# Layer 0's decays with chunk and head on 128 partitions and a chunk's 128 tokens along them

## The chip, the cores and the metric

The kernel runs on one core of one Trainium2 chip. The metric is the device time of one execution in microseconds (us), as the median of several runs. A core has five engines that work side by side, each through its own queue in a fixed order: PE (TensorE, matmuls; its weight loads are shown as PEld), DVE (VectorE), ACT (ScalarE), POOL (GpSimd) and SP (SyncE, which here issues every DMA). On-chip memory has 128 partitions: an instruction of DVE, ACT or POOL works on up to 128 partitions at once and walks along the elements of each.

## The reference, cut to what matters

Two layers on an input `x` of 2 x 512 tokens of 512 numbers. Layer 0 is a gated linear attention with decays and a feed-forward layer, layer 1 a softmax attention and a mixer whose 4 x 4 matrices go through 50 Sinkhorn iterations. The change touches the decays of layer 0's attention alone (32 heads, chunks of 128 tokens, 4 chunks to a row of the batch):

```python
dt = jax.nn.softplus(hidden_states @ Win.T + dt_bias)      # [B, L, 32]
A = -jnp.exp(A_log_bias)
g = dt * A
gc = g.transpose(0, 2, 1).reshape(B, H, NC, CHUNK)
G = jnp.cumsum(gc, axis=-1)                                # within a chunk
...
decay = jnp.where(causal, jnp.exp(G[..., :, None] - G[..., None, :]), 0.0)
y_intra = jnp.einsum('bhnij,bhnjd->bhnid', scores * decay, xc)
Glast = G[..., -1:]
k_dec = kc * jnp.exp(Glast - G)[..., None]
cstates = jnp.einsum('bhnjd,bhnje->bhnde', k_dec, xc)
chunk_decay = jnp.exp(G[..., -1])
```

For each row of the batch, head and token the kernel needs `dt` (softplus of a small projection), the running sum `G` of `dt * A` within the chunk, `exp(Glast - G) * dt`, and for each chunk `exp(Glast)`.

## The kernel before

Tokens stand on partitions in tiles of 128, so a row of the batch is 4 chunks `c`. Weights come in 256 KB tiles (`raw`, four buffers), each is split by ACT (a rounded copy, L228) and POOL (the rest, L229) into two halves, and a product takes three matmul passes (L251). Layer 0's attention runs in units of (group of 4 heads, row of the batch, chunk), 64 in all; each does `scores`, `mix`, `state`, `gate`, `turn` and `project_out`, with the projections of the next group between them. Layer 1 follows, and the Sinkhorn chains close the kernel: two on POOL with their reciprocals on DVE, and one on DVE.

The program is written in the order of the text of `tile_adaln`, and a scheduler that knows the dependencies lays each engine's queue out anew. An engine then works through its queue strictly in that order. Which instruction stands where is therefore decided when the program is built, and an edit in one place can move others.

The head of the kernel (L353 to L371) loads `x`, the modulation weights, the identity, `Win`, `dt_bias` and `A_log`, all through SP. `decays(b)` is called once for each row of the batch (L1395 and L1400), between the loads and the first projections and scores:

- For each chunk the tokens are normalised, transposed (L200), scaled into `ht` (L203), split into `hh` (L209) and `hl` (L212), and `also` multiplies `ht` by `Win` (L392): 32 heads on 32 partitions, the chunk's 128 tokens at their place among the row's 512, in the PSUM tile `zps`.
- L399 to L409 work out softplus on tiles of 32 partitions and 512 elements: `z`, `e`, `u`, `rest`, `dt`, on DVE, with three exponentials and logarithms on ACT (L78 is the helper that records them).
- L412 multiplies by `-exp(A_log)`. The running sum goes in two levels: 15 additions within blocks of 16 tokens (L415, each on 32 x 32 elements: one token of every block), 7 additions over the 8 blocks of each chunk (L420, 32 x 4), and one that adds the offsets (L421).
- `G` is written to DRAM (L424, `g_dram`), from where `scores` loads four heads of a chunk, spread to all partitions (L512, `gb`, 256 KB, 64 of them). POOL masks it (L514), ACT takes the exponential, DVE multiplies it with the scores (L527), and PE reads the product in `mix` (L567).
- `exp(Glast)` (L427 to L431) goes to DRAM and comes back spread to all partitions as `cdb`, which `state` reads as a scalar for each head (L556, L557).
- L433 to L438 make `exp(Glast - G) * dt` and `-G`, and 12 transposes of 32 x 128 (L442) bring `-G`, `dt` and that product to token-major columns, which ACT copies into `gcol` (L443).

The temporary tiles come from the pool `wk` by name, two buffers to a name. The name `z` is also that of `mix`'s tile (L571).

Of the kernel before, what the change touches and what calls it, by code (L numbers as in the profile page):

```python
# [9 lines left out]
FP = mybir.dt.float32  # L10
# [22 lines left out]
ALU = mybir.AluOpType  # L33
# [3 lines left out]
P = 128  # L37
B, L, HID = 2, 512, 512
NC = L // P
KC = HID // P  # L40
H0, KV0, D0 = 32, 8, 128
REP0 = H0 // KV0
# [10 lines left out]
def tile_adaln(ctx: ExitStack, tc: tile.TileContext, a: dict, out: bass.AP):  # L53
    nc = tc.nc
# [3 lines left out]
    small = ctx.enter_context(tc.tile_pool(name="small", bufs=4))  # L58
    wk = ctx.enter_context(tc.tile_pool(name="wk", bufs=2))
    dram = ctx.enter_context(tc.tile_pool(name="dram", bufs=1, space=bass.MemoryType.DRAM))  # L60
    psp = ctx.enter_context(tc.tile_pool(name="ps", bufs=2, space=PSUM))
# [15 lines left out]
    def act(o, i, func, **kw):  # L77
        ins = nc.scalar.activation(o, i, func, **kw)  # L78
        tc.add_manual_dep(
            ins.ins, table.ins.name,  # L80
            mybir.DependencyInfo(mybir.DependencyClass.NoSync, mybir.DependencyReason.DATA),
            reason="the activation table",
        )
        return ins.ins
# [5 lines left out]
    def keep(shape):  # L90

        m = int(np.prod(shape[1:]))
        t = room0[0:shape[0], used0[0]:used0[0] + m]
        used0[0] += m
        if len(shape) == 2:
            return t
        names = "abc"[:len(shape) - 1]
        return t.rearrange(
            f"p ({' '.join(names)}) -> p {' '.join(names)}", **{n: k for n, k in zip(names, shape[1:])}
        )  # L100
# [36 lines left out]
    anchor = {}  # L137
# [33 lines left out]
    def temp(shape, dt, name, bufs=2):  # L171
        return wk.tile(shape, dt, name=name, bufs=bufs)
# [17 lines left out]
    def norm(src, root=rsqrt_pool):  # L190
        xn = temp([P, HID], FP, "xn")
        normalised(xn, src, root)
        return xn
# [167 lines left out]
    ident = keep([P, P])  # L361
    nc.sync.dma_start(out=ident, in_=a["c_ident"])
    win = keep([P, KC, H0])
    nc.sync.dma_start(out=win, in_=a["WinT"].rearrange("(k p) h -> p k h", p=P))
    dtb = keep([H0, 1])
    nc.sync.dma_start(out=dtb, in_=a["dt_bias"])
    alog = keep([H0, 1])
    nc.sync.dma_start(out=alog, in_=a["A_log"])
    act(alog, alog, AF.Exp)
    gn = keep([P, 1])  # L370
    nc.sync.dma_start(out=gn, in_=a["gnorm"])  # L371
# [8 lines left out]

    gcol = keep([P, 3, NC, B * H0])
    ngc, dtc, wdc = gcol[:, 0], gcol[:, 1], gcol[:, 2]
    cdb = keep([P, B * H0, NC])
    g_dram = [dram.tile([H0, L], FP, name=f"g_dram{b}") for b in range(B)]
    cd_dram = [dram.tile([H0, NC], FP, name=f"cd_dram{b}") for b in range(B)]
    def decays(b):

        zps = psp.tile([H0, L], FP, name="zps")

        def also(cs, ht):  # L390
            for kc in range(KC):
                nc.tensor.matmul(zps[:, cs], lhsT=win[:, kc, :], rhs=ht[:, kc, :], start=kc == 0, stop=kc == KC - 1)  # L392

        for c in range(NC):
            modulated(b, c, norm(xin[b * NC + c], rsqrt), modT[0], 0, also=also)

        row = lambda n: temp([H0, L], FP, n)
        z, e, u, rest, dt = row("z"), row("e"), row("u"), row("rest"), row("dt")
        nc.vector.tensor_scalar(z, zps, dtb, None, ALU.add)  # L399
        nc.vector.scalar_tensor_tensor(e, z, -1.0, z, ALU.mult, ALU.min)  # L400
        act(e, e, AF.Exp)

        nc.vector.tensor_scalar(u, e, 1.0, None, ALU.add)
        nc.vector.scalar_tensor_tensor(rest, u, -1.0, e, ALU.add, ALU.subtract)
        act(dt, u, AF.Ln)
        act(u, dt, AF.Exp, scale=-1.0)
        nc.vector.tensor_tensor(rest, rest, u, ALU.mult)
        nc.vector.tensor_tensor(dt, dt, rest, ALU.subtract)
        nc.vector.scalar_tensor_tensor(dt, z, 0.0, dt, ALU.max, ALU.add)  # L409

        G = row("G")
        nc.vector.tensor_scalar(G, dt, alog, -1.0, ALU.mult, ALU.mult)  # L412
        Gb = G.rearrange("r (n i) -> r n i", i=16)
        for i in range(1, 16):
            nc.vector.tensor_tensor(Gb[:, :, i], Gb[:, :, i], Gb[:, :, i - 1], ALU.add)  # L415
        off = small.tile([H0, NC, 8], FP, name="off")
        G4 = G.rearrange("r (c n i) -> r c n i", n=8, i=16)
        nc.vector.memset(off[:, :, 0], 0.0)
        for n in range(1, 8):
            nc.vector.tensor_tensor(off[:, :, n], off[:, :, n - 1], G4[:, :, n - 1, 15], ALU.add)  # L420
        nc.vector.tensor_tensor(  # L421
            Gb, Gb, off.rearrange("r c n -> r (c n)").unsqueeze(2).to_broadcast([H0, NC * 8, 16]), ALU.add
        )
        nc.sync.dma_start(out=g_dram[b], in_=G)  # L424
        Gc = G.rearrange("r (c i) -> r c i", c=NC)
        glast = small.tile([H0, NC], FP, name="glast")
        nc.vector.tensor_copy(glast, Gc[:, :, P - 1])  # L427
        cd = small.tile([H0, NC], FP, name="cd")
        act(cd, glast, AF.Exp)
        nc.sync.dma_start(out=cd_dram[b], in_=cd)  # L430
        nc.sync.dma_start(out=cdb[:, b * H0:(b + 1) * H0, :], in_=cd_dram[b].partition_broadcast(P))  # L431

        nc.vector.tensor_tensor(  # L433
            e.rearrange("r (c i) -> r c i", c=NC), Gc, glast.unsqueeze(2).to_broadcast([H0, NC, P]), ALU.subtract
        )
        act(e, e, AF.Exp, scale=-1.0)
        nc.vector.tensor_tensor(e, e, dt, ALU.mult)
        nc.vector.tensor_scalar(G, G, -1.0, None, ALU.mult)  # L438
        for k, src in enumerate((G, dt, e)):
            tp = psp.tile([P, NC, H0], FP, name="gtp")  # L440
            for c in range(NC):
                nc.tensor.transpose(tp[:, c, :], src[:, c * P:(c + 1) * P], ident[0:H0, 0:H0])  # L442
            nc.scalar.copy(gcol[:, k, :, b * H0:(b + 1) * H0], tp)  # L443


# [59 lines left out]
    def scores(u):  # L505

        g, b, c = u["at"]
        r0 = b * H0 + g * REP0
        q, kT = u["q"], u["kT"]
        gb = wk.tile(sh4, FP, name="gb", bufs=2)  # L510
        h0 = g * REP0
        anchor["sp"] = nc.sync.dma_start(out=gb, in_=g_dram[b][h0:h0 + REP0, c * P:(c + 1) * P].partition_broadcast(P)).ins  # L512
        dec = wk.tile(sh4, FP, name="dec", bufs=2)
        anchor["pool"] = nc.gpsimd.affine_select(  # L514
            out=dec, in_=gb, pattern=[[0, REP0], [1, P]], compare_op=ALU.is_ge, fill=-1e30,
            base=0, channel_multiplier=-1,
        ).ins
        for h in range(REP0):
            anchor["act"] = act(dec[:, h, :], dec[:, h, :], AF.Exp, bias=ngc[:, c, r0 + h:r0 + h + 1])
        sps = psp.tile(sh4, FP, name="sps", bufs=2)  # L520
        if "kh" in u:
            kh, kl = u["kh"]
            passes(sps, [((kh[:, c, :], kl[:, c, :]), exact(q[:, c], "q", sh4))])
        else:
            anchor["pe"] = nc.tensor.matmul(sps, lhsT=kT[:, c, :], rhs=q[:, c], start=True, stop=True).ins
        for h in range(REP0):
            anchor["dve"] = nc.vector.scalar_tensor_tensor(  # L527
                dec[:, h, :], sps[:, h, :], dtc[:, c, r0 + h:r0 + h + 1], dec[:, h, :], ALU.mult, ALU.mult
            ).ins
        u["pr"] = dec  # L530
        if c:
            u["qg"] = gb
            act(gb, gb, AF.Exp)
            nc.gpsimd.tensor_tensor(gb, gb, q[:, c], ALU.mult)  # L534

    def state(u, st):

        g, b, c = u["at"]
        r0 = b * H0 + g * REP0
        xw = wk.tile(sh4, FP, name="xw", bufs=2)  # L540
        nc.gpsimd.tensor_tensor(  # L541
            xw, u["v"][:, c, :].unsqueeze(1).to_broadcast(sh4),
            wdc[:, c, r0:r0 + REP0].unsqueeze(2).to_broadcast(sh4), ALU.mult,
        )
        cps = psp.tile(sh4, FP, name="cps", bufs=2)
        if type(u["kt"]) is tuple:
            kh, kl = u["kt"]
            passes(cps, [((kh[:, c, :], kl[:, c, :]), exact(xw, "xw", sh4))])
        else:
            nc.tensor.matmul(cps, lhsT=u["kt"][:, c, :], rhs=xw, start=True, stop=True)  # L550
        ns = wk.tile(sh4, FP, name="st", bufs=2)
        if c == 0:
            nc.scalar.copy(ns, cps)
        else:
            for h in range(REP0):
                nc.vector.scalar_tensor_tensor(  # L556
                    ns[:, h, :], st[:, h, :], cdb[:, r0 + h, c:c + 1], cps[:, h, :], ALU.mult, ALU.add  # L557
                )
        return ns

# [864 lines left out]
    for n, u in enumerate(units):  # L1425
        g, b, c = u["at"]
# [128 lines left out]
```

## Time and profile before

| what | value |
|---|---|
| median of 3 runs | 1373.19 us (1372.54 to 1374.4) |
| the profiled execution | 1368.2 us |
| its span, first to last instruction | 1366.4 us |
| PE busy | 1238.1 us, 91% |
| DVE busy | 1116.2 us, 82% |
| ACT busy | 842.4 us, 62% |
| POOL busy | 792.2 us, 58% |
| mean granted TensorE clock | 0.961 |
| DMA packets | 94,243, 109.81 MB |

The profile is of one execution, so sums over it are made against its own 1368.2 us. A busy PE is not a PE at its peak: matmuls are pipelined, so a 512-wide one is shown with some 390 ns while the next follows after 230 ns. A row of groups shows line, engine, operation, the tile written and those read, the shape (partitions x elements), the count, then the busy us and mean ns of one, and last the idle time of the engine before them with what ended it. In a view of waits a line shows who waited for whom: us in total, times, longest. An instruction's duration includes what it waits inside the engine after it has begun.

### The profile page before, as it was taken

Reading aid. Unit: us, or ns where it says so; the run is one execution under the profiler, and the core shown is the slowest. Engines: PE = TensorE matmul, PEld = TensorE weight load, DVE = VectorE, ACT = ScalarE, POOL = GpSimd, SP = SyncE. Lnnn points to the kernel's source line nnn. Section 1 sums busy time; section 2 is a strip of 40 time slices with the busy share of each in tenths; the row PEclk is TensorE's granted clock in tenths of the full one; section 3 lists DMA queues with packets and bytes.
Section 4 is the critical chain, followed back from the end, with each engine's and each line's share of the span. In section 5 each row is a group of like instructions: output and inputs, shape, how many; then the busy total and the mean of one; then the engine's idle time right before and its main releaser. Section 6 shows DMA issues by size and latency. Waiting matters only on the chain. (4 is left out here: it accounts for less than half of the span.)

```text
span 1366.4 us, 23105 instructions
## 1 busy us (share of the span) xinstructions
PE 1238.1 (91%) x7224; PEld 996.0 (73%) x7224; DVE 1116.2 (82%) x2732; ACT 842.4 (62%) x2378; POOL 792.2 (58%) x1233
## 2 busy tenths in 40 slices
PE   5989999999999999999999999889999999996408
PEld 2767788788788778888877787667777777764308
DVE  7999677786787777877989886788779888898887
ACT  4457476476465556666657675366758678875308
POOL 4455374265266356776788877545435855658651
PEclk9999999999999999999999999899999999997659
DMA  7122241232132233242343232623214221200001
GB/s 247 38 66 43 86 131 47 65 94 74 37 102 86 62 120 105 81 121 83 110 124 108 76 112 70 174 66 106 80 31 120 80 69 49 66 14 1 12 5 47
DMA packets 94243, 109.81 MB, mean 80 GB/s; under 512 B 13277, under 2 KB 52957, under 8 KB 94121
## 3 DMA queue, kind: packets, MB, share of 16 engines
q1 hardware_dynamic: 94120, 108.34, 27.0%
q8 instruction: 57, 0.93, 0.3%
q14 instruction: 66, 0.53, 0.1%
HBM read 100.02 MB, written 8.02 MB: 79 GB/s over the span
## 5 line engine op out<-in xcount | busy, mean ns | idle before, releaser
L870 DVE TENSOR_REDUCE m<-s 128x1 f32<-128x512 f32 x256 | 165.9, 672 | 13.4 <-PE s L866 12.7
L78 ACT ACTIVATE pt<-s 128x512 f32<-128x512 f32 x256 | 137.4, 601 | 13.0 <-PE s L904 12.0
L466 POOL TENSOR_TENSOR q<-xcos,rot 128x512 f32<-128x512 f32 x64 | 93.1, 1455 | 51.9 <-DVE xcos L464 49.2
L78 ACT ACTIVATE sg<-sg 128x512 f32<-128x512 f32 x128 | 80.9, 633 | 61.9 <-DVE sg L497 60.1
L866 PE MATMUL s<-ks,qs 96*128 96x512 f32 x256 | 104.1, 435 | 8.6 <-DVE m L870 7.2
L251 PE MATMUL pps<-hh,wq_h 128*128 128x512 f32 x256 | 103.1, 403 | 1.1 <-ACT vT L784 1.1
L251 PE MATMUL ops<-wo_h,zl 128*128 128x512 f32 x256 | 101.3, 396 | 1.0 <-DVE zl L590 0.9
L251 PE MATMUL ops<-wo_h,zh 128*128 128x512 f32 x256 | 101.3, 396 | 0.6 <-DVE zl L590 0.6
L251 PE MATMUL pps<-hl,wq_h 128*128 128x512 f32 x256 | 101.3, 396 | 0.0
L251 PE MATMUL gps<-wg_h,hh 128*128 128x512 f32 x256 | 101.1, 396 | 0.0
L534 POOL TENSOR_TENSOR gb<-gb,q 128x512 f32<-128x512 f32 x48 | 63.6, 1327 | 64.5 <-ACT gb L78 48.2
L251 PE MATMUL pps<-hh,wq_l 128*128 128x512 f32 x256 | 100.7, 394 | 0.0
L251 PE MATMUL gps<-wg_l,hh 128*128 128x512 f32 x256 | 100.7, 393 | 0.0
L904 PE MATMUL s<-qs,ks 100*128 100x256 f32 x512 | 98.9, 299 | 1.9 <-ACT pt L78 1.2
L567 PE MATMUL yps<-v,dec 128*128 128x128 f32 x512 | 94.2, 279 | 6.6 <-DVE xcos L464 2.7
L78 ACT ACTIVATE dec<-dec,room 128x128 f32<-128x128 f32 x256 | 82.7, 397 | 28.2 <-POOL dec L514 27.7
L251 PE MATMUL gps<-wg_h,hl 128*128 128x512 f32 x256 | 100.0, 391 | 0.0
L251 PE MATMUL ops<-wo_l,zh 128*128 128x512 f32 x256 | 100.0, 391 | 0.0
L514 POOL TENSOR_SCALAR_AFFINE_SELECT dec<-gb 128x512 f32<-128x512 f32 x64 | 48.4, 756 | 88.9 <-DMA gb<-g_dram 40.1
L904 PEld LDWEIGHTS s<-qs,ks 100*128 100x128 f32 x512 | 82.1, 193 | 18.3 <-ACT pt L78 5.4
L541 POOL TENSOR_TENSOR xw<-v,room 128x512 f32<-128x512 f32 x48 | 55.9, 1178 | 64.5 <-ACT v L481 64.5
L577 DVE SCALAR_TENSOR_TENSOR z<-yps,ss,sg 128x128 f32<-128x128 f32 x256 | 71.7, 342 | 26.4 <-ACT ss L78 26.0
(318 smaller groups left out, 3946.7 us busy)
## 6 DMA issues: line engine op xcount, KB each, us to landing
gb<-g_dram SPq DMA_DIRECT2D x64, 256.0 KB
raw<-in_wq SPq DMA_DIRECT2D x56, 256.0 KB
raw<-in_wg SPq DMA_DIRECT2D x48, 256.0 KB
raw<-in_wo SPq DMA_DIRECT2D x48, 256.0 KB
raw<-in_wmod SPq DMA_DIRECT2D x40, 256.0 KB
qs<-q_dram SPq DMA_DIRECT2D x64, 64.0 KB
raw<-in_wk SPq DMA_DIRECT2D x14, 256.0 KB
raw<-in_wv SPq DMA_DIRECT2D x14, 256.0 KB
```

The source lines that it names most:

```text
L78: ins = nc.scalar.activation(o, i, func, **kw)
L251: nc.tensor.matmul(ps, lhsT=l, rhs=r, start=i == 0, stop=i == n - 1)
L466: nc.gpsimd.tensor_tensor(dst, sp(xc_), sp(rot), ALU.add)
L514: anchor["pool"] = nc.gpsimd.affine_select(out=dec, in_=gb, pattern=[[0, REP0], [1, P]], compare_op=ALU.is_ge, fill=-1e30, base=0, channel ...
L534: nc.gpsimd.tensor_tensor(gb, gb, q[:, c], ALU.mult)
L541: nc.gpsimd.tensor_tensor(xw, u["v"][:, c, :].unsqueeze(1).to_broadcast(sh4), wdc[:, c, r0:r0 + REP0].unsqueeze(2).to_broadcast(sh4), ALU. ...
L567: nc.tensor.matmul(yps[:, h, :], lhsT=u["pr"][:, h, :], rhs=u["v"][:, c, :], start=True, stop=not c)
L577: nc.vector.scalar_tensor_tensor(z[:, h, :], yps[:, h, :], ss[:, h:h + 1], sg[:, h * P:(h + 1) * P], ALU.mult, ALU.mult)
L866: anchor["pe"] = nc.tensor.matmul(ps, lhsT=st["qs"][rp][0:KS, i, qt * P:(qt + 1) * P], rhs=st["ks"][s][0:KS], start=True, stop=True,).ins
L870: anchor["dve"] = nc.vector.tensor_reduce(st["m"][:, 2 * qt + s, i:i + 1], ps, AX.X, ALU.max, negate=True).ins
L904: nc.tensor.matmul(ps[:, j, :], lhsT=st["ks"][s][0:KM, kt * P:(kt + 1) * P], rhs=st["qs"][rp][0:KM, i, :], start=True, stop=True,)
```

## The change

`zps` and the temporary tiles become 128 partitions of 128 elements: partition `c * 32 + head`, a chunk's tokens along it. `also` writes the chunk's 32 heads to the partitions of the chunk, and `dt_bias` and `A_log` are loaded four times each, once for each chunk's partitions. Every DVE and ACT step of `decays` works on the new tiles; the 15 additions are on 128 x 8 elements, the 7 on 128 x 1. The step that subtracts `glast` takes it as a scalar for each partition. The 12 transposes of a row become 3 of 128 x 128. `g_dram` has a row for each chunk and head, so that four heads of a chunk lie next to each other; `cd_dram` and `cdb` have the chunk ahead of the head. The tiles get names of their own (`d_...`).

```diff
-    dtb = keep([H0, 1])
-    nc.sync.dma_start(out=dtb, in_=a["dt_bias"])
-    alog = keep([H0, 1])
-    nc.sync.dma_start(out=alog, in_=a["A_log"])
+    dtb, alog = keep([P, 1]), keep([P, 1])
+    for c in range(NC):
+        nc.sync.dma_start(out=dtb[c * H0:(c + 1) * H0], in_=a["dt_bias"])
+        nc.sync.dma_start(out=alog[c * H0:(c + 1) * H0], in_=a["A_log"])
...
-    cdb = keep([P, B * H0, NC])
-    g_dram = [dram.tile([H0, L], FP, name=f"g_dram{b}") for b in range(B)]
-    cd_dram = [dram.tile([H0, NC], FP, name=f"cd_dram{b}") for b in range(B)]
+    cdb = keep([P, NC, B * H0])
+    g_dram = [dram.tile([NC * H0, P], FP, name=f"g_dram{b}") for b in range(B)]
+    cd_dram = [dram.tile([NC, H0], FP, name=f"cd_dram{b}") for b in range(B)]
...
-        zps = psp.tile([H0, L], FP, name="zps")
+        zps = psp.tile([P, P], FP, name="zps")
...
-                nc.tensor.matmul(zps[:, cs], lhsT=win[:, kc, :], rhs=ht[:, kc, :], start=kc == 0, stop=kc == KC - 1)
+                nc.tensor.matmul(zps[cs.start // NC:cs.stop // NC], lhsT=win[:, kc, :], rhs=ht[:, kc, :], start=kc == 0, stop=kc == KC - 1)
...
-        row = lambda n: temp([H0, L], FP, n)
+        row = lambda n: temp([P, P], FP, f"d_{n}")
...
-        off = small.tile([H0, NC, 8], FP, name="off")
-        G4 = G.rearrange("r (c n i) -> r c n i", n=8, i=16)
-        nc.vector.memset(off[:, :, 0], 0.0)
+        off = small.tile([P, 8], FP, name="off")
+        nc.vector.memset(off[:, 0:1], 0.0)
         for n in range(1, 8):
-            nc.vector.tensor_tensor(off[:, :, n], off[:, :, n - 1], G4[:, :, n - 1, 15], ALU.add)
...
+            nc.vector.tensor_tensor(off[:, n:n + 1], off[:, n - 1:n], Gb[:, n - 1, 15:16], ALU.add)
+        nc.vector.tensor_tensor(Gb, Gb, off.unsqueeze(2).to_broadcast([P, 8, 16]), ALU.add)
         nc.sync.dma_start(out=g_dram[b], in_=G)
...
-        nc.sync.dma_start(out=cd_dram[b], in_=cd)
-        nc.sync.dma_start(out=cdb[:, b * H0:(b + 1) * H0, :], in_=cd_dram[b].partition_broadcast(P))
-
-        nc.vector.tensor_tensor(
-            e.rearrange("r (c i) -> r c i", c=NC), Gc, glast.unsqueeze(2).to_broadcast([H0, NC, P]), ALU.subtract
-        )
+        nc.sync.dma_start(out=cd_dram[b].rearrange("c (h o) -> (c h) o", o=1), in_=cd)
+        nc.sync.dma_start(out=cdb[:, :, b * H0:(b + 1) * H0], in_=cd_dram[b].partition_broadcast(P))
+
+        nc.vector.tensor_scalar(e, G, glast, None, ALU.subtract)
...
-            for c in range(NC):
-                nc.tensor.transpose(tp[:, c, :], src[:, c * P:(c + 1) * P], ident[0:H0, 0:H0])
+            nc.tensor.transpose(tp.rearrange("p c h -> p (c h)"), src, ident)
...
-        anchor["sp"] = nc.sync.dma_start(out=gb, in_=g_dram[b][h0:h0 + REP0, c * P:(c + 1) * P].partition_broadcast(P)).ins
+        anchor["sp"] = nc.sync.dma_start(out=gb, in_=g_dram[b][c * H0 + h0:c * H0 + h0 + REP0].partition_broadcast(P)).ins
...
-                    ns[:, h, :], st[:, h, :], cdb[:, r0 + h, c:c + 1], cps[:, h, :], ALU.mult, ALU.add
+                    ns[:, h, :], st[:, h, :], cdb[:, c, r0 + h:r0 + h + 1], cps[:, h, :], ALU.mult, ALU.add
```

More of the change, by code (lines that the diff above doesn't have):

```diff
@@ L415, in decays @@
             nc.vector.tensor_tensor(Gb[:, :, i], Gb[:, :, i], Gb[:, :, i - 1], ALU.add)
-        off = small.tile([H0, NC, 8], FP, name="off")
-        G4 = G.rearrange("r (c n i) -> r c n i", n=8, i=16)
-        nc.vector.memset(off[:, :, 0], 0.0)
+        off = small.tile([P, 8], FP, name="off")
+        nc.vector.memset(off[:, 0:1], 0.0)
         for n in range(1, 8):
-            nc.vector.tensor_tensor(off[:, :, n], off[:, :, n - 1], G4[:, :, n - 1, 15], ALU.add)
-        nc.vector.tensor_tensor(
-            Gb, Gb, off.rearrange("r c n -> r (c n)").unsqueeze(2).to_broadcast([H0, NC * 8, 16]), ALU.add
-        )
+            nc.vector.tensor_tensor(off[:, n:n + 1], off[:, n - 1:n], Gb[:, n - 1, 15:16], ALU.add)
+        nc.vector.tensor_tensor(Gb, Gb, off.unsqueeze(2).to_broadcast([P, 8, 16]), ALU.add)
         nc.sync.dma_start(out=g_dram[b], in_=G)
[L425 to L428, printed above, removed]
+        glast = small.tile([P, 1], FP, name="glast")
+        nc.vector.tensor_copy(glast, G[:, P - 1:P])
+        cd = small.tile([P, 1], FP, name="cd")
         act(cd, glast, AF.Exp)
-        nc.sync.dma_start(out=cd_dram[b], in_=cd)
-        nc.sync.dma_start(out=cdb[:, b * H0:(b + 1) * H0, :], in_=cd_dram[b].partition_broadcast(P))
-        nc.vector.tensor_tensor(
-            e.rearrange("r (c i) -> r c i", c=NC), Gc, glast.unsqueeze(2).to_broadcast([H0, NC, P]), ALU.subtract
-        )
+        nc.sync.dma_start(out=cd_dram[b].rearrange("c (h o) -> (c h) o", o=1), in_=cd)
+        nc.sync.dma_start(out=cdb[:, :, b * H0:(b + 1) * H0], in_=cd_dram[b].partition_broadcast(P))
+        nc.vector.tensor_scalar(e, G, glast, None, ALU.subtract)
         act(e, e, AF.Exp, scale=-1.0)
```

## The prediction

> **What bounds the kernel now.** I read the page first, then the busy time by stretches, then the waits of the stretch the change lies in, then VectorE's groups there. On the page PE is busy 91% of the span, so a saving on another engine counts only where PE stands idle. The stretches say where (columns: from and to, length, then busy us and instructions of PE, weight load, DVE, ACT, POOL, then granted TensorE clock, DMA share, GB/s):
>
> ```profile
> 32.00:77.70 45.70, 45.68 (x212) 35.47 (x212) 44.99 (x85) 20.56 (x42) 19.25 (x13) 0.96 0.18 52
> 77.70:106.00 28.30, 20.83 (x92) 16.08 (x93) 27.72 (x59) 14.31 (x41) 17.37 (x16) 0.88 0.22 57
> 106.00:130.00 24.00, 23.93 (x141) 20.15 (x141) 23.24 (x51) 19.07 (x66) 13.54 (x11) 1.00 0.28 59
> ...
> 200.00:300.00 100.00, 100.00 (x507) 81.42 (x506) 75.33 (x153) 57.37 (x169) 45.58 (x39) 1.00 0.23 69
> ```
>
> PE is full before 77.7 us and again after 106. Between them it misses 28.30 - 20.83 = 7.5 us, and there DVE is full (27.72 of 28.30). DVE sets that stretch. What PE waited for from 70 to 110 us:
>
> ```profile
> PE cps L251 <- DVE xcos L464: 2.1, 1, 2.1
> PE gtp L442 <- DVE G L438: 1.9, 1, 1.9
> PE yps L567 <- DVE off L420: 1.4, 1, 1.4
> PE pps L251 <- ACT vT L784: 1.1, 1, 1.1
> PE ztp L585 <- DVE dec L527: 0.9, 1, 0.9
> ```
>
> Together 7.4 us, 6.3 of it ended by DVE, twice by instructions of the decays themselves (L438, L420). The pause from 77.7 also costs clock: the TensorE clock granted from 80 to 84 us was 0.50, and eleven 512-wide matmuls followed each other at 0.43 us, where later ones take 0.23. That is 11 x 0.20 = 2.2 us. PE could thus win up to 7.4 + 2.2 = 9.6 us. From 106 us on a saving on DVE buys nothing by itself, but what was won is kept, since PE is full until about 500 us and later waits are between engines that all start earlier.
>
> **The change part by part.** *DVE.* The decays of one row are 12 wide instructions and 15 + 7 narrow ones; all keep their number. Rows from 29 to 118 us (count of both rows of the batch, busy us, mean ns):
>
> ```profile
> L415 DVE TENSOR_TENSOR G<-G 32x32 f32<-32x32 f32 x30 | 11.7, 391 | 0.5
> L420 DVE TENSOR_TENSOR off<-off,G 32x4 f32<-32x4 f32 x14 | 5.0, 356 | 0.1
> L407 DVE TENSOR_TENSOR rest<-rest,u 32x512 f32<-32x512 f32 x2 | 3.3, 1636 | 0.0
> L412 DVE TENSOR_SCALAR G<-dt,room 32x512 f32<-32x512 f32 x2 | 2.0, 982 | 0.0
> ...
> L408 DVE TENSOR_TENSOR dt<-dt,rest 32x512 f32<-32x512 f32 x2 | 1.4, 677 | 0.0
> L400 DVE SCALAR_TENSOR_TENSOR e<-z 32x512 f32<-32x512 f32 x2 | 1.4, 676 | 0.0
> ```
>
> A time here goes by elements per partition: 32x512 at L408 takes 677 ns, as 128x512 does elsewhere (L473, 672). So at 128 elements the prices are those of 128x128 rows: a tensor_tensor 0.28 us (L952, 276 ns, one input in PSUM), a scalar_tensor_tensor 0.33 (L527, 334 in the first 130 us). No 128x128 tensor_scalar exists; between 128x8 (L264, 0.16) and 32x512 (L403, 0.41) a straight line gives 0.22, and 0.29 from PSUM (L276 0.15, L399 0.73). Undisturbed savings per row of the batch: L399 0.73-0.29 = 0.44; the scalar_tensor_tensor steps L400, L404, L409 each 0.67-0.33 = 0.34; L407, L408, L421, L437 each 0.67-0.28 = 0.39; L403 0.19, L412 (0.46 at its fastest) 0.24, L438 0.18; L433 becomes a tensor_scalar, 0.67-0.22 = 0.45. Sum 0.44 + 1.02 + 1.56 + 0.61 + 0.45 = 4.1. L415 goes from 32 elements to 8: 0.20 to the 0.16 of a 128x8 tensor_tensor (L266), 15 x 0.04 = 0.6. L420 (0.148 at the median) goes from 4 to 1: nothing. That is 4.7 us a row, 9.4 for both.
>
> The means stand above the undisturbed times: 30 x (391 - 200) = 5.7 us at L415, 14 x (356 - 148) = 2.9 at L420, and about 3.4 at L407, L412 and L409. These are waits inside instructions, while POOL works. Since their number stays, I take them as staying; they are the upper end: if they go too, DVE saves 9.4 + 12.0 = 21.4, more than PE can use. The lower end is 8.2, the wide ones alone.
>
> The Trainium skill, "SBUF — State Buffer", section "SBUF: two separate sides", speaks against counting these waits: VectorE with two SBUF inputs and GpSimd hold one shared port pair by an exclusive lock for a whole instruction. By that a shorter DVE instruction waits as long for a GpSimd one as a longer one does, and the sum stays 9.4; L415's mean of 391 ns beside a minimum of 191 fits it.
>
> *How much reaches PE.* DVE's order is a queue, so savings add up from instruction to instruction. Before the pause at 77.7 us row 0 is through (4.7; its L438 is the releaser) and row 1 as far as L407 (0.44 + 0.34 + 0.19 + 0.34 + 0.39 = 1.7): 6.4 us, more than the 1.9 us pause at L438; vT's 1.1 us hang behind it (ACT's exp of gb waits for POOL, which waits for the gb load of the same G). So the first group closes: 1.9 + 1.1 + 2.2 of clock = 5.2. The second group, 2.1 + 0.9 + 1.4 = 4.4 us up to 106, is met by DVE 7.8 us ahead (6.4 plus L408, L409, L412, 0.39 + 0.34 + 0.24 = 1.0, plus eleven L415, 0.4), but PE asks 5.2 us earlier: 2.6 closes. Together 7.8.
>
> *PE.* Per row 12 transposes of 32x128 (L442) become 3 of 128x128. Row 1's lie where PE is full: G and dt, eight, take 0.7 us from 118.94 to 119.63, so twelve some 1.0; three 128x128 at L480's 0.60 for four take 0.45. Saved 0.55. Row 0's lie in the pause: nothing. The 32 zps matmuls (L392) keep number and size, only their output partitions change.
>
> *ACT.* Four 32x512 (0.63) per row become 128x128 (0.27, L573): 2.9 us on an engine busy 5 of 10 there; hidden behind PE, no gain of its own, counted at 0.
>
> *SP and the DMAs.* dt_bias and A_log are eight loads instead of two: six more issues at 0.33 to 0.43 us, 2.3 us of SP's time before 21 us. They stand before the loads of wq, wv and wg; wk and wq move behind the last wm and the identity. Queued behind them: ACT's casts (wk_h 12.17), POOL's differences, and through the four raw buffers SP again. Cover: ACT ended these casts at 15.59 and next worked at 18.59, 3.0 us. Uncovered it would cost 2.3; I take 1.0, because PE's order now puts six gate matmuls, which need wg, ahead of the first key matmuls (28.97).
>
> g_dram holds a chunk's four heads side by side, so each of the 64 gb loads is 128 pieces of 2 KB instead of 512 of 512 B (24,576 fewer of the page's 94,243 packets). POOL waited 40.1 us for gb, but PE waited only 1.7 us for POOL's gb from 110 us on. Between 0 and 1.7 us; I take 0, being hidden behind PE.
>
> The cd round trip gets smaller pieces: 4 B out, 128 B back. It was issued at 79.67 and first read by L556 at 107.18 (row 1: 112.5, read well after): 27 us of cover. Cost 0; were it late, DVE's st would stop, and PE's yps with it.
>
> The Trainium skill, "DMA: Bandwidth & Descriptors", section "Specifications", says that pieces under 512 B lose line rate to a read-modify-write. No price for four-byte pieces stands in this case's trace; by the rule this load slows, and the sum stays as long as the cover does.
>
> *Order.* The scheduler lays the program out anew, but the built programs differ only in about the first seventh of each engine's order, a few rows of the middle, and the two POOL chains (sinkhorn) of the last quarter, shifted by half an iteration. DVE's last chain starts and ends at the same places of its queue (rows 2315 to 2701 against 2314 to 2701).
>
> *Sum.* 7.8 + 0.5 - 1.0 = 7.3 us. The profiled execution took 1368.2 us (span 1366.4); it becomes 1360.9. It lies 5.0 us below the 1373.19 us median of the runs, whose least is 1372.54, so I subtract from the median: 1365.9 us, 0.53% less.
>
> **The rivals.**
> 1. *The pauses only change their owner* (no change). For it: DVE's waits for POOL (12 us) stay and PE's new order meets them elsewhere; POOL waited 15.8 us for xcos from 32 to 110 us. Against it: L438 and L420, two of the releasers, move far ahead in DVE's order. Only the transposes and a quarter of the 7.8 remain, less the loads: 0.5 + 2.0 - 1.0 = 1.5, 1371.7 us.
> 2. *More than the pauses.* POOL-held waits shrink too and the last pause closes: 9.6 + 0.5 and 1.7 of gb, 11.8: 1361.4 us.
> 3. *Slower: the last sinkhorn chain.* From 1240 us PE is no bound (54.71 of 126.4 us) and the four-tile chain on DVE is: 33 iterations, two halves each, every half with a reduce, a reciprocal and a product in series. If the new order puts one more reciprocal of the POOL chains (197 ns) ahead in each half, that is 66 x 0.197 = 13.0 us: 1365.9 + 13.0 = 1378.9 us. It decides once it takes 51 of the 66 halves. Against it: between its first and last four-tile step DVE's order holds 70 instructions of the other two chains now and 71 after.
> 4. *The change does not do what it says*: each instruction's time does not fall with 128 elements. Then nothing but the loads: about 1374. L527 at 334 ns beside L408's 677 speaks against it; I count it with the first.
>
> **How the numbers follow.** The forecast has 0.59, rival 1 (with 4) 0.16, rival 2 0.15, rival 3 0.10. The forecast's own range is 1363 to 1369.5: 7.8 may be 5.2 (the first group alone) or 9.6, the loads 0 to 2.3. The range from 1361 to 1371.9 adds rival 2 and the upper half of rival 1's cases. 0.2% is 2.7 us, about what a measurement of this kernel can tell from no change. Faster takes the forecast, rival 2 and a little of rival 1: 0.76. Same, between 1370.5 and 1375.9, the rest of rival 1: 0.14. Slower, rival 3: 0.10.
>
> **What would show it.** Right: the decays stand on 128 partitions, the wide ones are at 0.2 to 0.35 us, L415's kin at 0.16 at its fastest; PE's idle between 77 and 106 us falls below 2 us and the granted clock there stays 1.0; the first output projection comes some 7 us earlier and this lead is still there at 600 and at 1200 us. Wrong: PE's pauses stand at other lines in the same sum; the first pps after 30 us starts later than 29 us (loads); or the lead is there at 1200 us and gone at the end (sinkhorn).

## The result, and the profile after

The changed kernel is slower: 1382.66 us at the median (1382.24 to 1384.08) beside 1373.8 us (1372.54 to 1374.98) for the kernel before, a ratio of 1.0071 with a 95% interval of 1.0053 to 1.009. Beside the experiments it ran once more: 1387.63 us against 1372.48, 1.0107 (1.0081 to 1.0133). Forecast were 1365.9 us and a range of 1361.0 to 1371.9, so the time lies outside the range, on the other side of no change. The profiled execution took 1382.24 us, 14.0 more than the profiled one before (1368.2); the medians lie 8.9 us apart, for that execution was one of the faster ones of its kernel.

Where it goes is seen at the output projections. The 64 results of `project_out` leave PSUM one after the other; the 8th left at 195.8 us before and at 209.8 after, the 21st at 369.0 and 382.4, the 64th at 1026.7 and 1040.4. The lag of 14 us is complete by the 8th, and hardly anything is added or won after that.

Busy times of the same stretches as before, of the changed kernel (from and to, length, then busy us and instructions of PE, weight load, DVE, ACT, POOL, then granted TensorE clock, DMA share, GB/s):

```profile
32.00:77.70 45.70, 36.87 (x169) 27.49 (x168) 34.41 (x76) 14.26 (x35) 15.70 (x13) 0.91 0.24 50
77.70:106.00 28.30, 23.16 (x102) 17.63 (x102) 27.85 (x51) 16.72 (x49) 16.27 (x13) 0.84 0.13 40
106.00:130.00 24.00, 21.18 (x108) 17.71 (x108) 18.45 (x51) 13.97 (x50) 7.62 (x7) 0.95 0.14 40
200.00:300.00 100.00, 100.00 (x515) 81.73 (x514) 76.04 (x154) 57.04 (x165) 47.29 (x40) 1.00 0.25 75
```

The stretch up to 77.7 us, where PE had been full, now lacks 45.70 - 36.87 = 8.8 us of PE, and DVE is not full there either (34.41): both wait for something else. The pause of 77.7 to 106 fell only from 7.5 to 5.1 us, and the next 24 us miss 2.8. What PE waited for from 20 to 130 us (us in total, times, longest):

```profile
PE sps L251 <- ACT qh L466: 7.2, 1, 7.2
PE ps_tr L200 <- DVE xn L185: 4.6, 1, 4.6
PE cps L251 <- DVE d_G L416: 3.1, 1, 3.1
PE gps L251 <- ACT room L437: 2.8, 1, 2.8
```

The longest wait begins at 68.8 us. Follow it back: the first scores (`sps`) need `qh` from ACT, that needs the fourth `q` from POOL, and POOL's queue holds a mask ahead of it, `dec<-gb`, whose `gb` came late. POOL's waits, and then SP's, in the same 110 us:

```profile
POOL dec L508 <- DMA gb<-g_dram: 19.9, 3, 13.3
```

```profile
SPq L428 <- DMA cd_dram<-cd: 13.2, 2, 6.6
```

SP's issues from 60 to 76 us (start, length, line, what is moved; `room<-cd_dram` is the load of `cdb`):

```profile
61.06 0.33 SPq L422 DMA_DIRECT2D g_dram<-d_G  x1
61.70 0.33 SPq L427 DMA_DIRECT2D cd_dram<-cd  x1
62.62 1.75 SPq L506 DMA_DIRECT2D gb<-g_dram  x2
71.01 0.37 SPq L428 DMA_DIRECT2D room<-cd_dram  x1
74.14 0.32 SPq L506 DMA_DIRECT2D gb<-g_dram  x1
```

The write of the chunk decays leaves at 61.70, and the load that waits for its landing leaves 9.3 us later. In the kernel before these two stood 4.0 us apart in row 0 and 1.3 in row 1, and the first two loads of `gb` stood ahead of the write:

```profile
74.72 0.93 SPq L512 DMA_DIRECT2D gb<-g_dram  x2
75.70 0.50 SPq L430 DMA_DIRECT2D cd_dram<-cd  x1
...
79.67 0.33 SPq L431 DMA_DIRECT2D room<-cd_dram  x1
```

More than that, in the changed kernel the two loads of `gb` issued between write and load hardly move. The DMA view of 63 to 70 us, after the 128 pieces of 4 B have been sent:

```profile
DMA packets 35, 0.05 MB, mean 8 GB/s; under 512 B 9, under 2 KB 9, under 8 KB 35
```

256 packets of 2 KB were queued there and 26 moved in 7 us.

The undisturbed prices came out about as forecast. DVE's groups of the decays from 29 to 118 us (count of both rows, busy us, mean ns):

```profile
L416 DVE TENSOR_TENSOR d_G<-d_G 128x8 f32<-128x8 f32 x30 | 11.8, 394 | 0.5
L420 DVE TENSOR_TENSOR off<-off,d_G 128x1 f32<-128x1 f32 x14 | 4.9, 348 | 0.3
L413 DVE TENSOR_SCALAR d_G<-d_dt,room 128x128 f32<-128x128 f32 x2 | 2.6, 1303 | 0.1
...
L409 DVE TENSOR_TENSOR d_dt<-d_dt,d_rest 128x128 f32<-128x128 f32 x2 | 1.0, 502 | 0.0
L408 DVE TENSOR_TENSOR d_rest<-d_rest,d_u 128x128 f32<-128x128 f32 x2 | 0.9, 440 | 0.4 <-ACT d_u L78 0.4
...
L401 DVE SCALAR_TENSOR_TENSOR d_e<-d_z 128x128 f32<-128x128 f32 x2 | 0.6, 289 | 0.0
```

The scalar_tensor_tensor fell from 676 to 289 ns, the median of the wide steps is 0.29 us and the fastest L416 took 0.156. But L413, 0.98 us before, takes 1.30: what it waits for inside did not shrink.

### The profile page after: what moved, and what is told of

It reads as the page before. It is cut to its first block, busy times and chain, and to the rows that moved or that the text cites. A ratio compares the mean times of both kernels' runs of the same rounds, so it can differ in the third digit from the quotient of the medians.

```text
span 1380.4 us, 23054 instructions
## 1 busy us (share of the span) xinstructions
PE 1243.9 (90%) x7206; PEld 1000.2 (72%) x7206; DVE 1111.1 (80%) x2732; ACT 840.3 (61%) x2378; POOL 788.7 (57%) x1233
## 5 line engine op out<-in xcount | busy, mean ns | idle before, releaser
L467 DVE TENSOR_TENSOR ql<-q,qh 128x512 fp32r<-128x512 f32 x64 | 66.4, 1061 | 42.1 <-ACT qh L466 41.9
```

The source lines that it names most:

```text
L467: nc.vector.tensor_tensor(lo, src, hi.bitcast(FP), ALU.subtract)
```

## The experiments

Theory A: the write in four-byte pieces holds the DMA queue, and what stands behind it comes late. Rivals: B, the new order alone costs the time; C, the eight small loads at the start do; D, the layout's saving on DVE does not reach PE in any case. Each edit lets the scheduler lay out the program anew, except in the first experiment, whose instructions stand in the same order on PE, DVE, ACT and POOL as before; so their traces were read beside their times. In the table stands when the 8th output projection left PSUM in the profile, and the time against the kernel before in the same runs.

| kernel | 8th projection, us | median, us | before, us | ratio, 95% interval |
|---|---|---|---|---|
| before | 195.8 | | | |
| change, first / again | 209.8 / 214.8 | 1382.66 / 1387.63 | 1373.8 / 1372.48 | 1.0071 (1.0053 to 1.009) / 1.0107 (1.0081 to 1.0133) |
| e1_small_pieces | 197.3 | 1373.1 | 1372.34 | 0.9996 (0.9976 to 1.0016) |
| e2_two_loads | 212.9 | 1387.64 | 1372.34 | 1.0109 (1.0077 to 1.0141) |
| e3_cd_on_tensor | 199.7 | 1376.64 | 1372.34 | 1.0027 (1.0007 to 1.0048) |
| e4_both | 195.5 | 1374.81 | 1372.34 | 1.001 (0.9988 to 1.0032) |
| e5_one_piece | 191.6 | 1372.03 | 1372.45 | 0.999 (0.9971 to 1.001) |
| e6_sums_late | 192.0 | 1369.91 | 1372.45 | 0.9979 (0.9961 to 0.9998) |
| e7_scan | 187.1 | 1365.08 | 1372.45 | 0.9948 (0.9931 to 0.9966) |
| e8_scan_in_before | 195.4 | 1370.31 | 1372.45 | 0.9994 (0.9975 to 1.0013) |
| e9_write_behind | 204.8 | 1380.96 | 1372.48 | 1.0071 (1.0049 to 1.0093) |
| e10_piece_and_loads | 196.3 | 1373.63 | 1372.48 | 1.0015 (0.9998 to 1.0033) |
| e11_scan_late | 189.1 | 1368.78 | 1372.48 | 0.9973 (0.9953 to 0.9993) |
| e13_rotations_first | 193.9 | 1370.87 | 1373.5 | 0.9994 (0.9976 to 1.0011) |
| e14_scan_rotations_first | 187.0 | 1362.42 | 1373.5 | 0.9928 (0.9906 to 0.9949) |

Single executions of one kernel lie up to 8 us from their median, so a row is read by its interval. The lead or lag at the 8th projection, of one execution, agrees with the difference of the medians to within some 5 us in every row, so most of what an edit does here is decided by then. Not all of it shows at the end of a single execution: e5 leads by 4.2 us at the 8th projection and by 0.2 at the 64th; its granted clock in the two stretches from 800 to 1000 us was 0.93 and 0.92, that of the kernel before 0.95 and 0.97.

**e1_small_pieces.** The kernel before with the pieces of the change's round trip.

```diff
-    cd_dram = [dram.tile([H0, NC], FP, name=f"cd_dram{b}") for b in range(B)]
+    cd_dram = [dram.tile([NC, H0], FP, name=f"cd_dram{b}") for b in range(B)]
...
-        nc.sync.dma_start(out=cd_dram[b], in_=cd)
+        nc.sync.dma_start(out=cd_dram[b].rearrange("c h -> h c"), in_=cd)
```

> The kernel before with one thing of the change alone: the 128 chunk decays of a row leave VectorE's 32 partitions as 128 pieces of 4 B (32 of 16 B before) and come back as pieces of 128 B (512 B before). The order of the instructions on all engines is that of the kernel before. Theory A (the four-byte write lands late and holds what is queued behind it): the load of cdb, which SP issued 3.4 us after waiting in all, waits 6 us or more for each of the two writes, the next load of gb leaves 4 to 6 us later, and the time rises by 1 to 4 us, to 1375 to 1378. Theory B (the pieces are harmless, the order alone costs the time): SP waits no longer than before and the time stays within 1 us of 1373.8. Theory C (the eight small loads): as B.

SP's issues of row 0 and row 1 in its trace:

```profile
74.48 0.50 SPq L430 DMA_DIRECT2D cd_dram<-cd  x1
75.09 0.38 SPq L219 DMA_DIRECT2D raw<-in_wq  x1
81.53 0.36 SPq L431 DMA_DIRECT2D room<-cd_dram  x1
...
109.71 0.33 SPq L430 DMA_DIRECT2D cd_dram<-cd  x1
115.00 0.38 SPq L512 DMA_DIRECT2D gb<-g_dram  x1
118.01 0.38 SPq L431 DMA_DIRECT2D room<-cd_dram  x1
```

From write to load 7.1 and 8.3 us instead of 4.0 and 1.3, in an unchanged order: the pieces alone make the write land late. SP waited 8.5 us in all for it (3.4 before), 6.0 and 2.5, so the second wait fell short of the 6 us expected of each. The time did not move, against theory A's 1 to 4 us: in this order the loads of `gb` that PE needs first stand ahead of the write. What stands 0.6 us behind it in row 0 is a load of weights (`raw`, 128 pieces of 2 KB), and that was not held at all. The DMA view of 75 to 79 us:

```profile
DMA packets 1211, 0.73 MB, mean 182 GB/s; under 512 B 192, under 2 KB 1082, under 8 KB 1210
```

The 1210 - 1082 = 128 packets of 2 KB and more are that whole load. So a late landing alone costs nothing here, and not everything queued behind such a write stands still.

**e2_two_loads.** The changed kernel, the 32 values of `dt_bias` and `A_log` repeated four times by the host and loaded at once.

```diff
-    for c in range(NC):
-        nc.sync.dma_start(out=dtb[c * H0:(c + 1) * H0], in_=a["dt_bias"])
-        nc.sync.dma_start(out=alog[c * H0:(c + 1) * H0], in_=a["A_log"])
+    nc.sync.dma_start(out=dtb, in_=a["dt_bias"])
+    nc.sync.dma_start(out=alog, in_=a["A_log"])
```

> The changed kernel with dt_bias and A_log in one load of 128 values each, which the host repeats four times; nothing else. With two loads the order of PE begins like that of the kernel before again: the first key matmul stands ahead of the gate matmuls. Theory A (four-byte write): only the pause of 4.6 us at 25 to 30 us and some 2 us of half clock behind it go, the pauses from 70 us on stay: 1376 to 1379. Theory B or C (the order or the loads at the start are the whole of it): 1364 to 1368, as forecast for the change.

The pause of 4.6 us for row 1's normalised rows falls to 1.3, as expected, and no time is won: PE waits 12.7 us for rotations instead, SP 17.7 us for the write, and the ratio is that of the change itself. The 1387.64 us lie above every range given, theory A's too. Theory C falls.

**e3_cd_on_tensor** and **e4_both.** No round trip through DRAM; e4 adds the two loads of e2.

```diff
-        nc.sync.dma_start(out=cd_dram[b].rearrange("c (h o) -> (c h) o", o=1), in_=cd)
-        nc.sync.dma_start(out=cdb[:, :, b * H0:(b + 1) * H0], in_=cd_dram[b].partition_broadcast(P))
+        cps = psp.tile([P, NC, H0], FP, name="gtp")
+        nc.tensor.matmul(cps.rearrange("p c h -> p (c h)"), lhsT=cd.to_broadcast([P, P]), rhs=ident, start=True, stop=True)
+        nc.scalar.copy(cdb[:, :, b * H0:(b + 1) * H0], cps)
```

> The changed kernel without the round trip of the chunk decays through DRAM: one matmul of 128x128 with the identity lays them on all partitions, ScalarE copies them out. Eight loads as in the change, so PE's order begins with the gates. Theory A: SP no longer waits 13.2 us for the write, gb lands within 4 us of its issue, the pause of 7.2 us at 70 us goes and with it those of 4.6 and 2.8 us from 90 us on at least in part: 1369 to 1375, while the pause at 25 us stays. Theory B or C: 1380 to 1383, no change.

> Both: two loads and the chunk decays by TensorE. Theory A with the order at the start: the sum of both, 1362 to 1368, below both kernels, with PE's pauses from 20 to 130 us below those of the kernel before. If the layout itself brings nothing (theory D: DVE's savings do not reach PE), 1371 to 1374, as the kernel before.

With the round trip the 7.2 us pause goes; from 209.8 the 8th projection comes to 199.7, and the time to 1376.64, somewhat above theory A's range. Both edits together bring the kernel back to where it was before and not below it: e4's 1374.81 is just above theory D's 1371 to 1374. Its longest waits of PE from 20 to 130 us:

```profile
PE pps L251 <- DVE xcos L458: 5.3, 2, 3.3
PE ttp L474 <- DVE dec L521: 3.5, 1, 3.5
```

**e5_one_piece.** The round trip stays, but the decays leave as one row of 512 B.

```diff
+        rowp = psp.tile([P, NC, H0], FP, name="gtp")
+        nc.tensor.transpose(rowp.rearrange("p c h -> p (c h)")[0:1], cd, ident)
+        cdr = small.tile([1, NC * H0], FP, name="cdr")
+        nc.scalar.copy(cdr, rowp.rearrange("p c h -> p (c h)")[0:1])
-        nc.sync.dma_start(out=cd_dram[b].rearrange("c (h o) -> (c h) o", o=1), in_=cd)
+        nc.sync.dma_start(out=cd_dram[b].rearrange("c (o h) -> o (c h)", o=1), in_=cdr)
```

> The changed kernel, eight loads and round trip of the chunk decays kept, but TensorE turns the column of 128 decays into one row first, so that it leaves as one piece of 512 B instead of 128 of 4 B (the load back in pieces of 128 B stays). Theory A (the four-byte pieces of the write hold the queue): as with the decays laid out by TensorE, 1373 to 1378, SP's wait for the write falls from 13.2 us to 4 or less, and gb's first wait on POOL falls from 13.3 to below 6 us. Theory B2 (the round trip itself, or the order of SP's queue with the load of cdb in it, costs the time): 1380 to 1384, as the change.

This is the largest single step: 0.999 against the change's 1.0071 and 1.0107, some 11 to 16 us; the median, 1372.03, lies just below theory A's range. SP's wait for the write is 0.7 us, POOL's longest for `gb` 5.7. The first loads of `gb`, from 64 to 71 us of its trace:

```profile
DMA packets 415, 0.75 MB, mean 108 GB/s; under 512 B 49, under 2 KB 50, under 8 KB 414
```

415 packets in these 7 us, where the change moved 35. One thing moved beside the pieces: the row is ready later, so that the write stands behind three loads of `gb` and not ahead of two. The next run has the four-byte pieces behind two loads; behind all three they were not run, so e5 alone does not part the pieces from their place.

**e9_write_behind.** The change's own pieces, with the write behind two loads of `gb` (an order given to the scheduler), the load of `cdb` behind a third.

```diff
+            if n == 0:
+                chunk_decays(*d0)
+                chunk_decays(*d1)
...
+        tc.add_manual_dep(out_cd, anchor["sp"].name, order_only, reason="behind the second gb")
```

> The changed kernel with all its pieces, 128 of 4 B for the write and of 128 B for the load, but in SP's queue the write of the chunk decays stands behind the first two loads of gb and not ahead of them, and the load of cdb behind the third. POOL's order stays. Theory A1 (the four-byte write delays what the queue carries behind it, and it was the first gb loads that PE could not wait for): 1371 to 1377, POOL's wait for gb falls from 13.3 us at its longest to below 7. Theory A2 (the pieces cost their time wherever they stand): 1379 to 1384.

SP in its trace, and then the DMA views of 63 to 67 us and of 67 to 74:

```profile
62.50 1.56 SPq L510 DMA_DIRECT2D gb<-g_dram  x2
64.10 0.43 SPq L439 DMA_DIRECT2D cd_dram<-cd  x1
66.73 0.32 SPq L510 DMA_DIRECT2D gb<-g_dram  x1
73.30 0.37 SPq L441 DMA_DIRECT2D room<-cd_dram  x1
```

```profile
DMA packets 381, 0.52 MB, mean 131 GB/s; under 512 B 125, under 2 KB 125, under 8 KB 381
```

```profile
DMA packets 73, 0.05 MB, mean 6 GB/s; under 512 B 51, under 2 KB 51, under 8 KB 73
```

The two loads ahead of the write run through, and the silence begins behind it: now the third load of `gb` crawls. PE's stretch from 60 to 77.7 us is nearly whole again (16.00 us busy against 10.50). In row 1, though, another load of `gb` (112.13 us) follows the write (111.71) at once. The timeline shows what hangs on it, from engine to engine (start, length, instruction, in brackets the wait ahead of it):

```profile
124.84 0.64 POOL L512 TENSOR_SCALAR_AFFINE_SELECT dec<-gb 128x512 f32<-128x512 f32 x1 [10.25 <-DMA gb<-g_dram]
125.50 1.28 ACT L78 ACTIVATE dec<-dec,room 128x128 f32<-128x128 f32 x4 [7.16 <-POOL dec L512]
125.94 1.23 DVE L525 SCALAR_TENSOR_TENSOR dec<-sps,room,dec 128x128 f32<-128x128 f32 x4 [7.13 <-ACT dec L78]
127.31 2.04 PE L565 MATMUL yps<-v,dec 128*128 128x128 f32 x8 [3.77 <-DVE dec L525]
```

POOL's longest wait is so 10.2 us and not below 7, and the time, 1380.96 us, lies in theory A2's range and above A1's: 1.0071 against the change's 1.0107 in the same runs, with intervals that overlap a little. The wait moved to whichever `gb` load stood behind the write, from the first two to the third in row 0 and to the next one in row 1. Putting the write elsewhere in row 0 won a part of the cost at most.

**e12_change_again.** The changed kernel once more, beside e9, e10 and e11.

> The changed kernel itself, beside the others on this chip: 1379 to 1385, and in its profile the same pauses as in its first one (7.2 us for the first scores, 4.6 us for row 1's normalised rows).

1387.63 us, above the range; in its profile the scores wait 9.2 us and the normalised rows 4.6.

**e10_piece_and_loads.** e5 with the two loads.

> e5_one_piece with dt_bias and A_log in one load each, as in e2_two_loads. e5_one_piece still has PE's pause of 4.6 us at 25 to 30 us for row 1's normalised rows, and the half clock behind it. Theory F (the eight loads cost the layout this pause by the order that they bring): the pause goes and the time falls by 3 to 6 us to 1366 to 1369. Theory D2 (the pauses change owner): 1370 to 1374.

The pause at 25 us goes (1.3 us left), but 1.0015: nothing is won. Theory F falls, D2 holds. What took over, in the waits of its PE:

```profile
PE pps L251 <- DVE xcos L461: 5.8, 3, 3.3
PE gtp L427 <- DVE xcos L461: 2.6, 1, 2.6
```

**e6_sums_late** and **e13_rotations_first.** In e4, DVE runs all wide steps of row 0 and the multiplication by A ahead of the first rotation (`rot`, `xcos`); in the kernel before the first rotation stood ahead of most of them, and three ahead of the multiplication. e6 moves the second half of row 0's decays down in the program, e13 writes out the old order.

```diff
+        i_ = nc.vector.tensor_scalar(u, e, 1.0, None, ALU.add).ins
+        if b == 0:
+            tc.add_manual_dep(i_, roped[-1].name, order_only, reason="behind the rotation")
```

> e4_both with row 0's decays from the multiplication by A on put behind the four queries in the program, ahead of the values; row 1's as before. In e4_both DVE gave 11.3 us to the decays from 32 to 60 us (7.5 in the kernel before) and PE waited 5.3 us for rotated rows (xcos) there. Theory D1 (the saving was spent by order: row 0's decays run ahead of the rotations that PE waits for): this pause goes, 1368 to 1372. Theory D2 (the order doesn't matter, what is won is lost elsewhere up to 106 us): 1373 to 1377.

> e4_both with DVE's order of the kernel before written out at the start: row 0's decays from u on stand behind the rotation of the keys, from the multiplication by A on behind that of the second query. In e4_both all wide steps stood ahead of the first rotation, and PE waited 5.3 us for rotations from 32 to 60 us (0 in the kernel before). Theory D1 (order spends the saving): that pause goes, PE misses less than 1 us from 32 to 60, and what DVE saves shows from 77 to 106 us: 1366 to 1369. Theory D2 (the saving doesn't reach PE in any order): 1371 to 1375.

e6 lies in theory D1's range, but the pause for rotations fell only from 5.3 to 3.7 us, and the gain is not clear of noise (0.9979 against e4's 1.001, the intervals overlap). In e13 the pause for rotations went, as theory D1 wanted (PE 27.56 of 28 us from 32 to 60), but the time stays level, 0.9994. Its stretches from 77.7 and from 90 us, and its waits of PE:

```profile
77.70:90.00 12.30, 8.46 (x34) 6.25 (x32) 12.00 (x26) 4.78 (x17) 6.25 (x6) 0.86 0.13 44
90.00:106.00 16.00, 13.53 (x73) 11.47 (x74) 12.94 (x42) 11.24 (x43) 5.10 (x6) 0.89 0.14 38
```

```profile
PE yps L569 <- DVE dec L529: 3.2, 2, 2.8
PE ztp L587 <- DVE z L579: 2.1, 1, 2.1
```

6.3 us of PE are missing there (7.5 before the change), for other instructions, with DVE full to 90 us. Order decides where the pauses stand; their sum hardly changes. The median of 1370.87 lies between the two ranges, at the lower edge of D2's.

**e7_scan, e8_scan_in_before, e11_scan_late, e14_scan_rotations_first.** The running sum by one `tensor_tensor_scan` of 128x128 (e8: four of 32x128 a row) in place of 24 instructions; e7 on e4, e8 on the kernel before, e11 on e6, e14 on e13.

```diff
-        for i in range(1, 16):
-            nc.vector.tensor_tensor(Gb[:, :, i], Gb[:, :, i], Gb[:, :, i - 1], ALU.add)
...
+        nc.vector.tensor_tensor_scan(G, onesP, G, 0.0, ALU.mult, ALU.add)
```

> e4_both with the running sum of a row of the batch by one tensor_tensor_scan of 128x128 in place of its 24 instructions (15 of 128x8, 7 of 128x1, the offsets added, and a memset). They took some 8.5 us of DVE a row. Theory E (DVE's narrow steps, which the layout doesn't shorten, set the stretch up to 106 us): 15 us less of DVE, of which PE can use what it still misses, some 8: 1364 to 1368. Theory D2: order eats it again, because the masks of the first scores now stand ahead of all four queries on POOL: 1371 to 1377.

> The kernel before, heads on 32 partitions, with the running sums by four scans of 32x128 per row of the batch in place of 24 instructions. Theory E: DVE loses some 7 us per row, PE's pauses from 77 to 106 us close by 6 to 8 us: 1363 to 1367. Theory D2: 1370 to 1376.

> e7_scan with row 0's decays, from the multiplication by A on, behind the four queries in the program as in e6_sums_late. Theory D1 (order): another 2 to 4 us less, 1361 to 1364. Theory D2: with the scan the decays are too short to be in anything's way, 1364 to 1367.

> e7_scan with the same order. Theory D1: PE's 2.3 us from 32 to 60 us go too: 1361 to 1364. Theory D2 or one gain for both: 1364 to 1368, as e7_scan.

The scan in e7's DVE groups:

```profile
L415 DVE TENSOR_TENSOR_SCAN d_G<-room,d_G 128x128 f32<-128x128 f32 x2 | 1.0, 508 | 0.0
```

DVE's time for both rows' decays was 35.8 us before, 30.3 after, 29.9 in e4, 21.6 in e8 and 9.9 in e7. The scan alone in the old layout gives nothing that can be measured, the new layout alone gives nothing, both together give 0.9948 and, with the rotations first, 0.9928 (9.9 us), which beats both kernels. e7 met theory E, e8 missed it, e14 lies in D1's range; e11, where putting the sums late should have helped, is slower than e7 and above both of its ranges, so e6's gain is no rule. Busy time from 20 to 106 us, first of the kernel before, then of e14:

```profile
20.00:106.00 86.00, 74.16 (x350) 55.94 (x349) 84.71 (x179) 44.88 (x116) 44.14 (x34) 0.94 0.25 68
```

```profile
20.00:106.00 86.00, 80.36 (x405) 61.94 (x404) 77.08 (x167) 54.02 (x161) 46.46 (x38) 0.96 0.27 83
```

PE is 6.2 us busier there (the changed kernel: 67.46, 6.7 less), and DVE, at 77.08 of 86, is no longer full.

## Why the prediction was wrong, point by point

- **The cd round trip, the step that failed.** The prediction had "issued at 79.67 and first read by L556 at 107.18: 27 us of cover. Cost 0". Cover was counted for the reader of `cdb` alone, and 79.67 is the issue of the load back; the write had left at 75.70. The right question was what stands in the queue behind the write: two loads of `gb`, ahead of POOL's masks, ahead of the fourth `q`, ahead of the first scores. The new order had put the write ahead of them, and that order is fixed when the program is built. Against the change's two measurements, the write with its place in the queue costs 11 to 16 us by e5 and 6 to 11 us by e3, which has no such write: where 0 was forecast, as much as the whole forecast gain of 7.3 us or about it, and of the other sign.
- **DVE's saving, 9.4 us.** Saved were 35.8 - 30.3 = 5.5. The 30 narrow additions took 11.7 us before and 11.8 after (1.2 were to be saved; the median did fall, from 0.208 to 0.174), the 14 of the offsets 5.0 and 4.9, the other steps went from 19.1 to 13.6. What failed is the premise that the waits inside instructions stay. Without its 12.0 us of waits the decays took 35.8 - 12.0 = 23.8 us before; less the forecast 9.4 that is 14.4, and of the 30.3 measured 15.9 are then waits. The Trainium skill, "SBUF — State Buffer", "SBUF: two separate sides", says that a VectorE instruction which needs the port pair that it shares with GpSimd (one in a two-port mode, or with two SBUF inputs beside a GpSimd instruction that reads SBUF) waits out the whole of a GpSimd instruction that holds it. By that a wait doesn't shrink with the instruction. The traces agree: 15 of the decays' instructions before and 18 after took over 0.25 us more than the fastest of the same step in any run, and each of them overlaps a POOL instruction. L413 (1.30 us at the mean, 0.28 at its fastest, in e4) ended both times within 0.1 us of the end of one. How many meet one goes by the order: in e3, e5, e6 and e13 it was 14 or 15, the decays took 26.3 to 27.0 us, and the saving of 8.8 to 9.5 us is about the forecast one. Why an order meets more or fewer no run explains.
- **How much reaches PE, 7.8 us.** Without the four-byte write the layout gives 0.9979 (e6), 0.999 (e5), 0.9994 (e13), 1.001 (e4), 1.0015 (e10) and 1.0027 (e3): from 3 us won to 4 us lost, though in four of these six DVE saved what was forecast. This is the first rival's mechanism, pauses that change their owner, and the price it was given, 1.5 us, is about right for these kernels. The forecast took the releasers before 106 us one by one and closed each; but with DVE still full to 90 us what PE gets is set by all that DVE has to do, and behind DVE stand others. In e8 DVE lost 14 us, and PE then waited 3.2 us for `vT` from ACT.
- **SP's eight loads, 1.0 us.** They were to cost by late weights. They were not that late: DVE's longest wait for a load there was 0.4 us. But with them in the program the order came out otherwise: eight gate matmuls stand ahead of the first key matmul (none before), and row 1's first normalised rows left DVE at 29.6 us (26.9 before). PE waited 4.6 us for these rows, and the first key matmul came at 33.99 us (28.97 before), at half clock (0.50 granted from 30 to 34 us, matmuls 0.43 us apart). The prediction's sign for that, a first `pps` later than 29 us, was met, by another cause than the one it named. e2, e4 and e10 take this pause away, and against the same kernels with eight loads (e12, e3, e5) the time stays about level: 1.0109 against 1.0107, 1.001 against 1.0027, 1.0015 against 0.999. Other pauses take its place.
- **Order.** "Differs only in the first seventh" was right and no comfort: there the time is decided. What was put ahead of what (masks ahead of `q`, decays ahead of rotations, the write ahead of `gb`) was not priced.
- **The transposes (0.5 us), ACT (0) and gb's pieces (0)** could not be seen as terms of their own. Of `gb`, e5's and e9's first loads show 2 KB pieces moving well where no four-byte write is ahead of them.
- **The third rival, the last sinkhorn chain,** had the right sign by chance and the wrong place: the lag was 13.4 us at the 21st projection, 13.7 at the 64th and 14.0 at the end.

The other signs: prices on 128 partitions right; PE's idle from 77 to 106 us below 2 us wrong (5.1); the granted clock there 1.0 wrong (0.84); the first output projection 7 us earlier half right (112.7 against 117.7), but the third was already 9 us later.

## What to carry to other kernels

When a transfer's pieces shrink, ask what is queued behind it and who waits for that, not only who reads it. Count cover for the queue, in the order of the built program. And where one engine is full over a stretch, a saving on it is worth the pauses only down to the next engine's chain: two cuts that give nothing singly (the layout, the scan) gave 0.5% together.

## What the hardware showed that was not expected

After a write of 512 B in 128 pieces of 4 B, one from each partition, the load that waits for it was issued 7.1 to 11.2 us later, for both rows in the five traces with this write (the change twice, e1, e2, e9). 32 pieces of 16 B took 4.0 and 1.3 us by the same measure in the kernel before, one piece of 512 B 1.1 us in row 0 of e5 (in row 1 another issue stood between) and 1.5 and 1.1 us in e10. The measure goes from issue to issue, so it holds what the write waits in its queue too; but in the change's row 0 the pieces, shown with 0.01 us each, were out by 63 us and the load left at 71.01, so there the time lies after the sending.

Where loads of `gb` stood close behind this write (row 0 of the change, twice, and of e2, both rows of e9), they hardly moved for 7 us and more. The load of weights close behind it in e1's row 0 did move, its packets in among the write's own. What parts these cases no run shows.

The Trainium skill, "DMA: Bandwidth & Descriptors", "Specifications", says that pieces under 512 B bring a read-modify-write; the first two forms are under it and the third is not, but the first two differ by a factor of two and more, so the threshold alone doesn't price them. The same page, "Back-pressure in remote DMA", says that stalled writes also stall the other queues of their DMA engine, and speaks of transfers between cores. What e9 shows of loads behind a write to DRAM, in one queue, resembles it; whether it is the same mechanism, no run here shows.

Open remain this mechanism; how much of the cost is the pieces' and how much their place's, since neither the four-byte write behind all three first loads of `gb` nor one piece ahead of them was run; why e3 (1.0027) stands a little above e5 (0.999), and e11 above e7; and which chain sets the start next, once the scan and the layout are both in.
